# Two graph layers on one core: the exponential of layer 0's source terms moved ahead of their spreading, and a lag of three blocks with eight weight buffers in layer 1

## The chip, the cores and the metric

The kernel runs on one core of a Trainium2 chip. A core has a matrix engine (TensorE, PE in the profile, with its weight loads listed apart as PEld), a vector engine (VectorE, DVE), a scalar engine (ScalarE, ACT), GpSimd (POOL) and SyncE (SP), which only issues transfers here. Each runs its own list of instructions in order, and they wait for each other through semaphores. The metric is the device time of one execution in microseconds (us). Before the change the median of three runs is 3651.67 us (3650.04 to 3655.39).

## The reference, cut to what matters

For 16 graphs of 1024 nodes with 256 features, two layers run one after the other.

```python
# layer 0: 4 heads of 64, one adjacency type in use (adj is 0 or 1)
h      = x @ W                                     # per head
weight = leaky_relu(e_src[i] + e_dst[j], 0.01)     # where adj is 1, else -1e9
dst    = softmax(weight) @ h + bias
out    = head_norm(relu(dst) + h);  x = layer_norm(x + out)
# layer 1: 8 heads of 32, q = k = v = the normalised x
normed = layer_norm(x) * gamma1 + beta1
attn   = softmax(where(adj > 0, normed @ normed.T / sqrt(32), -inf))
y      = x + attn @ normed
y      = y + gelu(layer_norm(y) @ W1 + b1) @ W2 + b2
x      = layer_norm(x + y)
```

In layer 0 the weight before the softmax depends on a source term and a destination term only. exp(leaky_relu(s + d)) is, up to a factor for each destination that is put into the values, the larger of exp(0.99 s) and exp(-0.99 d). So the kernel never takes an exponential of a full 1024 x 1024 matrix in layer 0: it takes those of the terms and forms a maximum. Layer 1 does take an exponential for every pair of nodes and head.

## The kernel before, in words

The 16 graphs ("batches") go through two streams of work. `layer0` (L728) prepares batch b+1 and runs its attention while `layer1` (L745) runs attention and the MLP of batch b. Both are Python generators; every `yield` gives a cost in units of the author's planner. The loop at L789 takes the next piece of layer 0 when its progress is behind what `wanted` (L776) asks for at the present point of layer 1, else the next piece of layer 1. Short side jobs ("chains", such as a normalisation) are begun with a waiting time (`begin`, L270) and resumed by `advance` (L280) once that many units have passed; `complete` (L286) runs what is left of one at once. The order in which the four engines issue is the order in which this program emits; nothing is reordered later. The sums use `ATTN1` (L772), the units of layer 1's attention, so they change if that number does.

**Layer 0.** `prepare` (L312) takes two blocks of 128 nodes at a time: it transposes x (L253), turns the adjacency into a byte mask (L321 on PE, L322 on ACT), forms h and the two terms in one product (L348), and takes from it, on ACT, the source terms (`apart`, L349), the exponentials of the destination terms (L350, L351) and the scaled values (L353). `take_h` (L373, a chain begun 1.5 units after L348) copies h out of the PSUM bank on DVE, and with that the bank is free. `turn_sources` (L365) transposes the source terms and copies them to `esr` (L369).

`attention0` (L376) runs 16 steps for each batch. `spread_factor` (L383) multiplies a row of `esr` with a matrix of ones, so that the source term of every node lies on all 128 partitions (L389), in two PSUM banks of the pool `ps_s`; ACT takes the exponential of them (L391) into `cb`. There are four such pairs for a batch. `weights` makes the masked maximum (L400, DVE), `products` multiplies it with the values (L415, PE). `after0` (L458) is a long chain of normalisations; its last part needs GpSimd for a power (L224), then DVE (L234, L501, L502), then ACT (L240), and ends with transposes (L515, which profile as L253 on PE and L259 on ACT) into nT and with the values v1 (L520) of layer 1. The transposes use banks of the pool `ps_a` (two banks, `acc`), which L321, L348, L253, L368 and L619 share.

**Layer 1.** `attention1` (L528) has 32 steps per batch: two halves of queries, two groups of four heads, eight blocks of 128 keys. Step i is:

- `exponentials(i)`: four products for the logits (L543, below "QK"), one in each of the four banks of `ps_s`, and four exponentials on ACT (L548) into two buffers of the pool `six`;
- `masked(i-1)`: two multiplications with the mask on DVE (L554);
- `products(i-2)` (below "PV"): two heads with the values as the stationary operand (L561), two with the weights as the stationary operand (L568).

The 2 in the last line is `LAG` (L576). The first `LAG` steps cost 1.0 unit each, all others 2.5, and at the end `LAG` more steps have products but no logits. Step 4 is the first to need the second half of the keys. If layer 0's chain for that half has not ended by then, `half` calls `finish_norms` (L722), which completes it on the spot, ahead of QK4.

`heads_out` (L600) divides by the sums, `finish1` (L625) normalises (L630 to L646), `mlp` (L655) runs the two matrix products with a Gelu between (L663, L670, L676), and `last_norm` (L704) normalises once more and writes the result out.

**Buffers.** Pools have a fixed number of buffers for each name: `six` has 6 of the masked weights p, `three` 3 of v1, `four` 4 of z, `two` 2 of relu. A tile that finds no free buffer makes its first writer wait for the last reader of the tile before.

Of the kernel before, what the change touches and what calls it, by code (L numbers as in the profile page):

```python
# [31 lines left out]
F32 = mybir.dt.float32  # L32
# [3 lines left out]
AF = mybir.ActivationFunctionType  # L36
# [3 lines left out]
P = 128  # L40
# [10 lines left out]
def fast_path(  # L51
# [24 lines left out]
    nc = tc.nc  # L76
    B, N, D = x.shape
    H0, _, HO = w0.shape
    T = a_src.shape[2]
    DFF = w1.shape[1]  # L80
    H1 = 8
    HD = D // H1
    NB = N // P
    DC = D // P
    FC = DFF // P
    HALF = 512
    NH = N // HALF
    BPH = HALF // P
    Q = 32
    TILE = 64  # L90
    PAIR = 2
    GB = 2
    QUAD = 4
# [6 lines left out]
    one = ctx.enter_context(tc.tile_pool(name="one", bufs=1))  # L100
    two = ctx.enter_context(tc.tile_pool(name="two", bufs=2))
    three = ctx.enter_context(tc.tile_pool(name="three", bufs=3))
    four = ctx.enter_context(tc.tile_pool(name="four", bufs=4))
    six = ctx.enter_context(tc.tile_pool(name="six", bufs=6))
    small = ctx.enter_context(tc.tile_pool(name="small", bufs=3))
    ps_s = ctx.enter_context(tc.tile_pool(name="ps_s", bufs=4, space=PSUM))
    ps_a = ctx.enter_context(tc.tile_pool(name="ps_a", bufs=2, space=PSUM))
# [62 lines left out]
    bias0_r = rows(nc.scalar, bias0, "bias0_r")  # L170
    for i, (_, _, dst) in enumerate(terms):
        for c in range(DC):
            t = two.tile([P, H0, HO], F32, name="z")
            for pair in range(H0 // PAIR):
                heads = slice(pair * PAIR, (pair + 1) * PAIR)
                nc.vector.tensor_mul(
                    t[:, heads, :],
                    w0e[:, c, pair * P : (pair + 1) * P].rearrange("p (h e) -> p h e", e=HO),
                    vectors[i * PAIR + pair][:, :, :, 0],
                )  # L180
            nc.vector.tensor_reduce(dst[:, c, :], t, axis=mybir.AxisListType.X, op=OP.add)
# [60 lines left out]
    def side_bank(shape):  # L242

        if place[1][1] < ATTN1:
            return ps_a.tile(shape, F32, name="acc")
# [119 lines left out]
    def turn_sources(dst):  # L365
        es = ps_a.tile([P, GB, P], F32, name="acc")
        for g in range(GB):
            nc.tensor.transpose(es[:, g, :], apart[g].rearrange("p h q -> p (h q)"), ident)  # L368
        nc.scalar.copy(dst, es.rearrange("p g q -> p (g q)"))  # L369
        yield from ()  # L370

    def take_h(h, ph):
# [3 lines left out]
    def attention0(b, hb, v0, esr, dinv, factors, mask, rinv):  # L376

        groups = [(n, pair) for n in range(NH) for pair in range(H0 // PAIR)]  # L380
        steps = [(n, hd, j4) for n in range(NH) for hd in range(H0) for j4 in range(0, NB, 4)]

        def spread_factor(n, pair):  # L383

            cb = two.tile([P, PAIR, HALF], F32, name="cb")
            pbs = [ps_s.tile([P, HALF], F32, name="ps") for _ in range(PAIR)]
            for e in range(PAIR):
                q = slice((pair * PAIR + e) * Q, (pair * PAIR + e + 1) * Q)
                nc.tensor.matmul(pbs[e], spread[q, :], esr[q, n * HALF : (n + 1) * HALF], start=True, stop=True)  # L389
            for e in range(PAIR):  # L390
                nc.scalar.activation(cb[:, e, :], pbs[e], AF.Exp, scale=0.99)  # L391
            return cb

        def weights(n, hd, j4):
            ps = []
            cb = cbs[n, hd // PAIR]
            for j2 in (j4, j4 + 2):
                p = four.tile([P, 2, HALF], F32, name="p0")
                for i in range(2):
                    nc.vector.scalar_tensor_tensor(  # L400
                        p[:, i, :],
                        cb[:, hd % PAIR, :],
                        dinv[:, j2 + i, hd : hd + 1],
                        mask[n][:, j2 + i, :],
                        op0=OP.max,
                        op1=OP.mult,
                    )
                ps.append(p)
            return ps

        def products(ps, hd, j4, av):
            for i in range(4):
                for q in range(BPH):
                    for at in range(0, P, TILE):
                        nc.tensor.matmul(  # L415
                            av[at : at + TILE, q, :],
                            ps[i // 2][:, i % 2, q * P + at : q * P + at + TILE],
                            v0[:, j4 + i, hd, :],
                            start=j4 + i == 0 and q == 0,
                            stop=j4 + i == NB - 1 and q == BPH - 1,  # L420
                        )

        cbs = {groups[0]: spread_factor(*groups[0])}
        yield 1.0
        nc.vector.tensor_copy(factors, v0[:, :, :, HO])
        ps = weights(*steps[0])
        yield 1.0
        for i, (n, hd, j4) in enumerate(steps):
            if j4 == 0:
                av = ps_a.tile([P, BPH, HO + 1], F32, name="acc")  # L430
            products(ps, hd, j4, av)
            if i + 1 < len(steps):
                ps = weights(*steps[i + 1])
            if j4 == 0 and i + 3 < len(steps) and hd % PAIR == PAIR - 1:
                g = steps[i + 3][0], steps[i + 3][1] // PAIR
                cbs[g] = spread_factor(*g)
            if j4 == NB - 4:
                norms[b, n, hd] = after0(b, n, hd, av, hb[n], rinv[:, n * BPH : (n + 1) * BPH, :])
                begin(norms[b, n, hd], 2.5)
            yield 2.0  # L440

    def relu_residual(av, hd, hb, rinv):

        nc.vector.reciprocal(rinv[:, :, hd], av[:, :, HO])  # L444
        t = two.tile([P, BPH, HO], F32, name="relu")
        for q in range(BPH):
            nc.vector.scalar_tensor_tensor(
                t[:, q, :],
                av[:, q, 0:HO],
                rinv[:, q, hd : hd + 1],  # L450
                nbias0_r[:, hd * HO : (hd + 1) * HO],
                op0=OP.mult,
                op1=OP.max,
            )
        h = hb[:, :, hd * HO : (hd + 1) * HO]
        nc.vector.tensor_add(h, h, t)

    def after0(b, n, hd, av, o, rinv):  # L458
# [40 lines left out]
        t = minus_mean(mv[:, :, 0], r2[:, 0:BPH], BPH)  # L499
# [14 lines left out]
        for g in range(0, BPH, GB):  # L514
            transpose_rows(nT[:, :, g * P : (g + GB) * P], normed[:, g : g + GB, :], g1_c, be1_c)  # L515
            yield 1.5
        v1 = three.tile([P, BPH, H1, HD + 1], F32, name="v1")
        nc.vector.memset(v1[:, :, :, HD], 1.0)
        for g in range(BPH):
            nc.vector.tensor_mul(  # L520
# [7 lines left out]
    def attention1(half, mask, rinv, done):  # L528
# [8 lines left out]
        def exponentials(n, quad, jb):  # L537
            keys = slice(jb % BPH * P, (jb % BPH + 1) * P)
            of_keys, of_queries = half(jb // BPH)[2], half(n)[2]
            tiles = [ps_s.tile([P, HALF], F32, name="ps") for _ in range(QUAD)]  # L540
            for e in range(QUAD):
                q = slice(e * HD, (e + 1) * HD)
                nc.tensor.matmul(tiles[e], of_keys[q, quad, keys], of_queries[q, quad, :], start=True, stop=True)  # L543
            ps = []
            for e in range(0, QUAD, PAIR):
                p = six.tile([P, PAIR, HALF], F32, name="p")
                for i in range(PAIR):
                    nc.scalar.activation(p[:, i, :], tiles[e + i], AF.Exp, scale=SCALE1)  # L548
                ps.append(p)
            return ps  # L550
# [22 lines left out]
                            stop=jb == NB - 1 and e == PAIR - 1 and q == BPH - 1,  # L573
                        )

        LAG = 2  # L576
        ready = {}
        for i in range(len(steps) + LAG):
            if i < len(steps):
                ready[i] = exponentials(*steps[i])  # L580
            if 0 <= i - 1 < len(steps):
                masked(*steps[i - 1], ready[i - 1])
            if i < LAG:
                yield 1.0
                continue
            n, quad, jb = steps[i - LAG]
            if jb == 0:
                moved = ps_o.tile([P, HALF], F32, name="po")
                held = ps_o.tile([P, BPH, PAIR, HD + 1], F32, name="po")
            products(quad, jb, ready.pop(i - LAG), moved, held)  # L590
            if jb == NB - 1:
# [110 lines left out]
            yield 3.5  # L702

    def last_norm(b, k, po, x1):  # L704
        z = four.tile([P, 1, D], F32, name="z")
        nc.vector.tensor_add(z[:, 0, :], po, x1)
        mv = small.tile([P, 2], F32, name="mv")
        statistics(z[:, 0, :], mv)
        v = small.tile([P, 1], F32, name="v")
        nc.vector.tensor_scalar(v, mv[:, 1:2], EPS, None, op0=OP.add)  # L710
        r = power(v, 1, "r")
        yield 3.5
        t = minus_mean(mv[:, 0:1], r, 1)
        yield 1.5
        scale_shift(z, z, t, r, 1)
        nc.sync.dma_start(out[b, k * P : (k + 1) * P, :], z[:, 0, :])
# [52 lines left out]


    WORK0 = NB // GB * 3.25 + 2.0 + NB * H0 // 2 * 2.0
    ATTN1 = 2.0 + 2.5 * (NH * NB * H1 // QUAD)  # L772
    WORK1 = ATTN1 + NB // GB * (1.75 * FC / 2 + 3.5 * GB)
    COURSE = [(0.0, 1.0), (ATTN1, 1.45), (WORK1 - 14.0, 2.0), (WORK1, 2.0)]

# [469 lines left out]
```

## Time and profile before

One execution was profiled. Its own time and its span, from the first to the last instruction, stand beside the runs:

| | us |
|---|---|
| runs, median (lowest to highest) | 3651.67 (3650.04 to 3655.39) |
| profiled execution, own time | 3651.19 |
| its span | 3649.4 |
| PE busy | 3449.4 |
| DVE busy | 2988.7 |
| ACT busy | 2155.9 |
| POOL busy | 384.4 |
| ACT table loads: before L670, L391, L548, L256 | 46, 30, 15, 1 times 1.283 each |

A line of the costliest groups reads: source line, engine, operation, names of what is written and read, shape, how often; then busy time in us and mean ns of one; then the engine's idle time just before, and what ended it. In the chain of waits, a line names who waited for whom: us in total, times, longest. A line of the timeline gives start, duration, engine, source line, operation, how many were merged, and in brackets the idle time before it with its releaser. A line of the table by stages gives the stretch, its length, then busy us with the number of instructions for PE, PEld, DVE, ACT and POOL, then the clock granted to TensorE, the share of the DMA engines, and GB/s. The ends of matmuls are modelled: a matmul that waits behind another counts as busy, so the busy time of PE holds stalls too.

### The profile page before, as it was taken

How to read it: one execution, taken by the hardware profiler on the slowest of the kernel's cores; microseconds unless marked ns; L12 is line 12 of the kernel's file. 1: busy time of each engine (PE TensorE's matmuls, PEld its weight loads, DVE VectorE, ACT ScalarE, POOL GpSimd, SP SyncE). 2: the span in 40 equal slices, each digit the busy share in tenths (PEclk: the TensorE clock that was granted, in tenths of full speed). 3: DMA queues.
4: the chain of work that ended last, by engine and by line, in shares of the span. 5: the costliest groups of instructions: out<-in, count | busy, mean ns of one | idle time of the engine just before them, and what ended most of it. 6: DMA issues, size and time to landing. Idle time of an engine off the chain costs nothing.

```text
span 3649.4 us, 142033 instructions
## 1 busy us (share of the span) xinstructions
PE 3449.4 (95%) x64417; PEld 2302.3 (63%) x64417; DVE 2988.7 (82%) x5332; ACT 2155.9 (59%) x4732; POOL 384.4 (11%) x360
## 2 busy tenths in 40 slices
PE   6699999999999999999999999999999999999998
PEld 5457576675756757566584765757567575665846
DVE  5788887888878888798887978888788887888884
ACT  3564746647475573755738466474664747557464
POOL 0102011010110101101010010101101011010110
PEclk9899999999999999999999999999999999999999
DMA  4100201011020110201102010020201102010000
GB/s 105 35 16 26 36 12 40 13 30 32 14 43 10 34 27 15 44 9 36 23 16 46 8 42 15 26 36 13 41 11 31 31 14 46 7 38 9 15 7 14
DMA packets 77814, 97.55 MB, mean 27 GB/s; under 512 B 9104, under 2 KB 60048, under 8 KB 77200
## 3 DMA queue, kind: packets, MB, share of 16 engines
q0 software_dynamic: 18432, 33.56, 6.5%
q1 hardware_dynamic: 57184, 53.76, 4.8%
q8 instruction: 506, 8.29, 0.9%
q10 hardware_dynamic: 1584, 1.05, 0.1%
q14 instruction: 108, 0.88, 0.1%
HBM read 105.13 MB, written 16.78 MB: 33 GB/s over the span
## 4 chain that ended last, share of the span: by engine, by line
PE 64%; DVE 25%; issue 4%; ACT 3%; POOL 3%; DMA 1%; SPq 0%; ACTq 0%; POOLq 0%; DVEq 0%
PE ps L543 13%; PE po L561 10%; PE ps L663 9%; PE acc L415 9%; DVE p L554 7%; PE po L676 7%; PE po L568 6%; DVE p L400 6%; PE acc L348 3%; POOL r L224 3%; DVE st L229 2%; PE acc L321 1%; PE acc L253 1%; PE ps L389 1%; DVE mv L230 1%
## 5 line engine op out<-in xcount | busy, mean ns | idle before, releaser
L554 DVE TENSOR_TENSOR p<-p,mask 128x1024 f32<-128x1024 f32 x1024 | 1199.3, 1218 | 161.2 <-ACT p L548 157.3
L548 ACT ACTIVATE p<-ps 128x512 f32<-128x512 f32 x2048 | 1059.6, 614 | 331.7 <-PE ps L543 329.9
L543 PE MATMUL ps<-nT 32*128 32x512 f32 x4096 | 770.1, 655 | 12.6 <-ACT cb L391 10.0
L400 DVE SCALAR_TENSOR_TENSOR p<-cb,dinv,mask 128x512 f32<-128x512 f32 x1024 | 698.5, 744 | 0.9 <-ACT cb L391 0.9
L568 PEld LDWEIGHTS po<-v,p 128*32 128x32 f32 x32768 | 389.4, 109 | 335.0 <-issue 239.3
L415 PE MATMUL acc<-v,p 128*64 128x65 f32 x16384 | 556.1, 226 | 42.1 <-DVE p L400 40.1
L415 PEld LDWEIGHTS acc<-v,p 128*64 128x64 f32 x16384 | 512.0, 139 | 114.3 <-DVE p L400 61.6
L670 ACT ACTIVATE hid<-ps,b_sb 128x256 f32<-128x256 f32 x512 | 235.5, 471 | 556.9 <-PE ps L663 556.5
L561 PE MATMUL po<-p,v 128*32 128x512 f32 x2048 | 548.3, 610 | 10.5 <-DVE p L554 8.8
L561 PE MATMUL po<-p,unit 128*32 128x512 f32 x2048 | 547.9, 610 | 0.0
L663 PE MATMUL ps<-yT,w_sb 128*128 128x256 f32 x2048 | 491.0, 387 | 0.4 <-issue 0.4
L676 PE MATMUL po<-w_sb,hid 128*128 128x256 f32 x2048 | 465.0, 381 | 0.0
L676 PEld LDWEIGHTS po<-w_sb,hid 128*128 128x128 f32 x2048 | 385.4, 190 | 64.0 <-issue 11.4
L663 PEld LDWEIGHTS ps<-yT,w_sb 128*128 128x128 f32 x2048 | 375.6, 190 | 64.9 <-issue 13.1
L568 PE MATMUL po<-v,p 128*32 128x33 f32 x32768 | 387.7, 198 | 9.5 <-issue 4.3
L543 PEld LDWEIGHTS ps<-nT 32*128 32x128 f32 x4096 | 268.2, 186 | 171.1 <-issue 56.9
L561 PEld LDWEIGHTS po<-p,v 128*32 128x32 f32 x2048 | 78.6, 109 | 388.3 <-DVE p L554 206.1
L224 POOL TENSOR_TENSOR r<-v,mhalf 128x1 f32<-128x1 f32 (+1 forms) x160 | 158.1, 988 | 1009.1 <-DVE v L710 721.6
L348 PE MATMUL acc<-w0e,xT 128*128 128x264 f32 x512 | 146.4, 409 | 29.5 <-DVE hb L373 20.9
L322 ACT ACTIVATE mask<-acc,shift_c 128x1024 uint8<-128x1024 bf16 x128 | 144.3, 1127 | 43.6 <-PE acc L321 42.8
L304 POOL DMA_DIRECT2D ak<-in_adj_dram x128 | 69.7, 544 | 862.7 <-PE acc L321 840.3
L224 POOL TENSOR_TENSOR r<-v1s,mhalf 128x4 f32<-128x4 f32 x32 | 34.9, 1090 | 1134.6 <-DVE ranges L444 894.6
(117 smaller groups left out, 2927.9 us busy)
## 6 DMA issues: line engine op xcount, KB each, us to landing
ak<-in_adj_dram POOLq DMA_DIRECT2D x128, 256.0 KB, 3.9
xk<-in_x_dram SPq DMA_DIRECT2D x64, 256.0 KB, 2.8
xl<-in_x_dram SPq DMA_DIRECT2D x32, 512.0 KB, 4.0
out_dram<-z SPq DMA_DIRECT2D x128, 128.0 KB, 1.7
w_sb<-in_L_gnn_W_dram SPq DMA_DIRECT2D x2, 1024.0 KB, 8.0
v<-in_L_gnn_a_src_dram SPq DMA_DIRECT2D x2, 320.0 KB, 4.8
v<-in_L_gnn_a_dst_dram ACTq DMA_DIRECT2D x1, 320.0 KB, 5.0
xl<-in_L_gnn_a_dst_dram ACTq DMA_DIRECT2D x1, 320.0 KB, 5.3
```

Source lines behind the costliest of these rows:

```text
L224: nc.gpsimd.tensor_tensor(r, src, mhalf[:, :n], op=OP.pow)
L348: nc.tensor.matmul(ph, xT[:, c, g * P : (g + 1) * P], w0e[:, c, :], start=c == 0, stop=c == DC - 1)
L400: nc.vector.scalar_tensor_tensor(p[:, i, :], cb[:, hd % PAIR, :], dinv[:, j2 + i, hd : hd + 1], mask[n][:, j2 + i, :], op0=OP.max, op1=OP. ...
L415: nc.tensor.matmul(av[at : at + TILE, q, :], ps[i // 2][:, i % 2, q * P + at : q * P + at + TILE], v0[:, j4 + i, hd, :], start=j4 + i == 0 ...
L543: nc.tensor.matmul(tiles[e], of_keys[q, quad, keys], of_queries[q, quad, :], start=True, stop=True)
L548: nc.scalar.activation(p[:, i, :], tiles[e + i], AF.Exp, scale=SCALE1)
L554: nc.vector.tensor_mul(p, p, mask[n][:, jb, None, :].to_broadcast([P, PAIR, HALF]))
L561: nc.tensor.matmul(moved[at * Q : (at + 1) * Q, :], v, ps[0][:, e, :], start=jb == 0, stop=jb == NB - 1)
L568: nc.tensor.matmul(held[at : at + Q, q, e, :], ps[1][:, e, q * P + at : q * P + at + Q], values[:, hd, :], start=jb == 0 and e == 0 and q ...
L663: nc.tensor.matmul(ph, w1_sb[:, c, f * P : (f + 1) * P], yT[:, c, q * P : (q + GB) * P], start=c == 0, stop=c == DC - 1,)
L670: nc.scalar.activation(hid[f // 4][:, f % 4, :], ph, AF.Gelu, bias=b1_sb[:, f : f + 1], scale=1.0)
L676: nc.tensor.matmul(po, hid[f // 4][:, f % 4, g * P : (g + 1) * P], w2_sb[:, f, :], start=f == 0, stop=f == FC - 1,)
```

## The change

1. In `turn_sources` the copy of the transposed source terms to `esr` becomes an exponential with scale 0.99; in `spread_factor` the exponential becomes a copy. Since the spreading only repeats a row, the result in `cb` stands for the same quantity.
2. In `attention1`, `LAG` becomes 3: step i now multiplies the weights of step i-3. The pool of masked weights gets 8 buffers of 4 KB on each partition rather than 6. `ATTN1` becomes 3.0 + 2.5 x 32 = 83 rather than 82.
3. To make room, v1 gets 2 buffers rather than 3, relu 1 rather than 2, and z 3 rather than 4; the z of the start, which had its own two, shares those of `last_norm`.

```diff
-    six = ctx.enter_context(tc.tile_pool(name="six", bufs=6))
+    eight = ctx.enter_context(tc.tile_pool(name="eight", bufs=8))
...
-            t = two.tile([P, H0, HO], F32, name="z")
+            t = three.tile([P, H0, HO], F32, name="z")
...
-        nc.scalar.copy(dst, es.rearrange("p g q -> p (g q)"))
+        nc.scalar.activation(dst, es.rearrange("p g q -> p (g q)"), AF.Exp, scale=0.99)
...
-                nc.scalar.activation(cb[:, e, :], pbs[e], AF.Exp, scale=0.99)
+                nc.scalar.copy(cb[:, e, :], pbs[e])
...
-        t = two.tile([P, BPH, HO], F32, name="relu")
+        t = one.tile([P, BPH, HO], F32, name="relu")
...
-        v1 = three.tile([P, BPH, H1, HD + 1], F32, name="v1")
+        v1 = two.tile([P, BPH, H1, HD + 1], F32, name="v1")
...
-                p = six.tile([P, PAIR, HALF], F32, name="p")
+                p = eight.tile([P, PAIR, HALF], F32, name="p")
...
-        LAG = 2
+        LAG = 3
...
-        z = four.tile([P, 1, D], F32, name="z")
+        z = three.tile([P, 1, D], F32, name="z")
...
-    ATTN1 = 2.0 + 2.5 * (NH * NB * H1 // QUAD)
+    ATTN1 = 3.0 + 2.5 * (NH * NB * H1 // QUAD)
```

## The prediction

> **What bounds the kernel now.** Page first, then the waits, then one batch in order of time.
>
> ```profile
> PE 3449.4 (95%) x64417; PEld 2302.3 (63%) x64417; DVE 2988.7 (82%) x5332; ACT 2155.9 (59%) x4732; POOL 384.4 (11%) x360
> L554 DVE TENSOR_TENSOR p<-p,mask 128x1024 f32<-128x1024 f32 x1024 | 1199.3, 1218 | 161.2 <-ACT p L548 157.3
> L548 ACT ACTIVATE p<-ps 128x512 f32<-128x512 f32 x2048 | 1059.6, 614 | 331.7 <-PE ps L543 329.9
> L543 PE MATMUL ps<-nT 32*128 32x512 f32 x4096 | 770.1, 655 | 12.6 <-ACT cb L391 10.0
> ```
>
> TensorE looks full, but not all of it is work. 512 steps of L543 (logits, "QK") take 1.50 us each, while an unhindered one takes 1.07.
>
> ```profile
> PE acc L253 <- ACT sq L240: 53.4, 17, 11.0
> PE acc L415 <- DVE p L400: 40.1, 21, 5.0
> PE acc L348 <- DVE hb L373: 20.9, 19, 1.1
> PE po L561 <- DVE p L554: 8.8, 18, 1.7
> ```
>
> The longer lag aims at the last line, PE waiting for masked weights: 8.8 us in all. The others come from layer 0 and from the hand-over between the layers. The TensorE timeline at one hand-over (a batch takes some 222.5 us):
>
> ```profile
> 1249.53 2.59 PE L543 MATMUL ps<-nT 32*128 32x512 f32 x8
> 1252.60 1.97 PE L543 MATMUL ps<-nT 32*128 32x512 f32 x8
> ...
> 1256.05 1.16 PE L348 MATMUL acc<-w0e,xT 128*128 128x264 f32 x4
> 1257.14 1.14 PE L543 MATMUL ps<-nT 32*128 32x512 f32 x8
> ...
> 1259.54 0.77 PE L568 MATMUL po<-v,p 128*32 128x33 f32 x64
> 1262.59 1.92 PE L253 MATMUL acc<-ident,sq 128*128 128x128 f32 x8 [2.28 <-ACT sq L240]
> 1264.52 1.14 PE L543 MATMUL ps<-nT 32*128 32x512 f32 x8
> ```
>
> QK1 and QK2 (2.59, 1.97) hold TensorE because the banks of the previous step are freed only by its four exponentials. Then PE stands 2.28 us for the last piece of layer 0, which step 4 needs. Busy time late in the same attention:
>
> ```profile
> 1319.00:1340.00 21.00, 19.52 (x424) 9.83 (x425) 18.91 (x31) 16.68 (x40) 1.60 (x2) 1.00 0.16 26
> 1340.00:1360.00 20.00, 19.81 (x548) 11.33 (x544) 19.93 (x25) 11.54 (x23) 0.00 (x0) 1.00 0.02 4
> ```
>
> The third column of busy time is VectorE: 19.93 of 20 us. It has no gap from 1321 to 1372, so here two engines run neck and neck.
>
> [...] only L548, L391, L670 and the first L256 are preceded by a load. [...] the rows show 1283, and a load starting 0.01 us after the copy before it, so I use 1.28. [...] in the 15 us from 1030 that hold another hand-over the clock was 0.89.
>
> **Part 1: exponential ahead of spreading.** L391 becomes a copy: 592 ns now, copies of the same size take 594 (L256) and 612 (L603): nothing. L369 becomes an exponential: 371 ns as a copy; a 128x256 Gelu takes 471 (L670), so 0 to 0.1 us x 64, at most 6 us of ACT, beside TensorE; I take 0. Gone are 30 loads before L391 and, Gelu staying loaded, 30 of the 46 before L670: 60 x 1.283 = 77 us of ACT. On the end I value them at 0: ScalarE is idle there. In the MLP the load at 1175.70 is followed by 1.18 us more of waiting for L389, and after the second spread's pair of loads ScalarE waits 4.35 us for L663. No L663 shows a stall there over 0.1 us. The ends: 0 and 77 us.
>
> **Part 2: buffers.** Weights: exp(i) needed products(i-3) done, now i-4; either way TensorE issues those before QK(i): 0. relu has writer and reader on DVE in order: 0. z with three: lives from L706 to its landed write, 1237.46 to about 1244.5; the next L706 are at 1246.01 and 1250.20, so a fourth meets a free one. v1 with two: its last reader ends near 1377, the same half's next write comes with the following batch's layer 0 (as L520 at 1264.5): 0. Were the covers gone, L706 or L518 would hold the masks behind them on DVE, a few us a batch.
>
> **Part 3: the lag, through the planner.** The third start-up step now costs 1.0 rather than 2.5, ATTN1 is 83, so layer 0's pieces fall elsewhere. I followed the planner's sums (they give the timeline's order for before) and then walked PE, ACT and DVE with these durations: QK 1.07, products (PV) 1.56, L321 0.46, L348 1.08, L619 0.59, L415 2.02, four exponentials 2.06, L322 1.1, L349 to L353 1.07, a masked pair 2.36; a QK that waits ends 1.11 after the previous step's exponentials (QK6: 1272.04 to 1273.15).
>
> *Hand-over, before:* QK2, PV0, L348, QK3, PV1, wait, L253 x8, QK4. *After:* QK2, QK3, PV0, L348, wait, L253 x4, L253 x4, QK4. With times from QK0's start (1247.72):
> - QK3 directly follows QK2 at 6.8; exp(2) ends at 9.17 (1256.89), so QK3 ends at 10.3: stall 2.4, was 0.2.
> - PV0 and L348 end at 12.9. The VectorE chain behind L240 sits behind mask(1) and mask(2) as before (to 14.3), so L253 starts at 15.1: wait 2.2, was 2.4 (with 0.3 beside it).
> - L373 of that L348 is now emitted after the transposes; its bank is held, and the second four transposes must take the bank of the first, after L259 (two of about 0.5 us): 17.6. Stall 1.4, was 0. QK4 at 18.2, was 16.8.
>
> Stalls of TensorE in us, from the timeline (before) and the walk (after):
> - Steps 0 to 4: 1.45+0.83+0.19+0.26+2.37 = 5.1; after 1.45+0.83+2.42+2.2+1.4 = 8.3.
> - Steps 5 to 17: 0.81+0.66+0.22+0.66+0.81 = 3.2; after 0.21+0.22+0.30+0.17+0.31+0.76 = 2.0. L321 and L348 now fall in different steps, so fewer steps come bare.
> - Steps 18 to 31: 0.50 + 1.29 (L348 behind L373, itself behind the statistics of L630) + 1.54 + 1.37 (the first spread) + 0.98 + 0.63 + 1.2 (QK31 behind the second spread) = 7.5; after 0.17+0.76+1.3+0.73+0.60 = 3.6. L373 now goes ahead of L630, and the second spread comes after QK31.
>
> Sum 15.8 against 13.9: 1.9 us less per batch. VectorE allows it barely: L609 starts at 78.4 in the walk, with 47.6 us queued to the last mask, so its second half ends at 127.1 and the last PV at 128.0 (before 129.4). Nothing is saved twice: the last PVs carry the product displaced at the start. The MLP's order is unchanged.
>
> 15 batches x 1.9 = 28. The last batch has no layer 0 beside it, so only the lost cover at the start and one product more at the end: +2. Profiled execution 3651.2 (span 3649.4 and 1.8 around it; the median 3651.67 is 0.5 higher): 3651.2 - 26 = 3625.
>
> **Rivals.**
> *A. Slower: the hand-over bank.* The second four transposes get the bank that L373 holds. L373 then stands behind L510, L520 and mask(3) on VectorE and ends at 21.1 rather than 17.5; QK4 waits behind the transposes, and its exponentials with it. For: L348 already waits for L373 (20.9 us, 19 times). Against: at 1324.17 an L321 took the bank freed first, not the oldest. Price 3.5 x 15 = 52: 3678. It decides once the extra wait exceeds the 1.9 gained.
> *B. No change: VectorE paces the tail.* From 1321 it has no gap, so a TensorE freed of stalls waits for masks instead. Against: two masks fewer follow the L630 statistics. 3650.
> *C. The table loads count.* If ScalarE held TensorE in the MLP, 77 us would go: 3574. Against: L670 waits 556.5 us for L663, not the reverse.
> That the lag alone removes mask waits is worth at most the 8.8 us above.
>
> **Chances.** My forecast 0.45, A 0.22, B 0.15, C 0.08, the rest 0.10 (0.06 slower, 0.04 faster). A measurement tells about 0.2% (7 us) from no change: faster 0.45+0.08+0.04 = 0.57, same 0.15, slower 0.22+0.06 = 0.28. The forecast's own range is 3600 to 3642 (a misjudged stall of 1.5 us per batch). To hold 8 in 10 it runs from 3580, short of C, to 3682, past A.
>
> **What would show it.** Right: no load before L391 and 16 before L670; QK3 near 3.5 us long; the eight transposes split by about 1.4 us; PE waiting for L373 far below 20.9; the second spread after the last QK. The sum is wrong if QK4 comes later than 19 after QK0, if L561 waits for L554 more than now, or if the clock sinks at the longer hand-over (each us at half clock costs 0.5).

## The result: 1.0 % slower, and the profile after

The changed kernel takes 3685.93 us (median; 3683.30 to 3694.91) against 3651.07 us for the kernel before: a ratio of 1.0098, 95 % interval [1.0078, 1.0117]. The forecast was 3625, its range ended at 3682. The profiled execution of the changed kernel took 3694.91 us, its span 3693.0; it is the longest of those measured, so sums against it run some 9 us above the median.

The page of the changed kernel, busy times first, then the costliest groups:

```profile
PE 3485.5 (94%) x64417; PEld 2321.3 (63%) x64417; DVE 2990.1 (81%) x5332; ACT 2088.7 (57%) x4672; POOL 398.3 (11%) x360
L554 DVE TENSOR_TENSOR p<-p,mask 128x1024 f32<-128x1024 f32 x1024 | 1201.7, 1219 | 174.6 <-ACT p L548 173.6
L548 ACT ACTIVATE p<-ps 128x512 f32<-128x512 f32 x2048 | 1060.7, 615 | 329.7 <-PE ps L543 327.3
L543 PE MATMUL ps<-nT 32*128 32x512 f32 x4096 | 749.2, 664 | 17.1 <-ACT p L548 15.3
```

TensorE is busy 36 us longer with the same 64417 matmuls, while VectorE's time is what it was and ScalarE has 67 us less. L543 itself fell from 770.1 to 749.2: the logits do wait less. So something else made other matmuls longer: L561, for one, takes 632 ns each where it took 610. The chain of waits, TensorE's own, in us in total, times, longest:

```profile
PE acc L253 <- ACT sq L240: 46.4, 17, 9.8
PE acc L415 <- DVE p L400: 41.0, 22, 5.0
PE acc L253 <- ACT nT L259: 22.5, 16, 1.4
PE po L568 <- DVE o L610: 17.2, 15, 1.2
PE ps L543 <- ACT p L548: 15.3, 17, 1.0
...
PE acc L348 <- DVE hb L373: 4.3, 4, 1.3
```

L561's wait for L554 has gone from 8.8 us to at most 0.1, L348's for L373 from 20.9 to 4.3. Three lines are new or have grown: the second four transposes behind L259 (foreseen, 1.4 us each), QK3 behind the previous exponentials (foreseen, though largely as a stall inside the matmul), and L568 behind L610 (not foreseen). All three together are 55 us, where they were 5 before, while the lines that shrank gave back 42 us (16.6 at L348, 10.0 at L543 behind L391, 8.8 at L561, 7.0 at L253 behind L240). So the waits of TensorE grew by some 8 us, far less than the 36 us by which its busy time grew. What made the same matmuls longer shows in the clock. First a line of the groups by line, on part 1:

```profile
L670 ACT ACT_TABLE_LOAD x16 | 20.5, 1283 | 0.3
```

Part 1 did what it says: 16 loads ahead of L670 instead of 46, and none ahead of L391, which has no row of loads any more. The TensorE timeline of one hand-over (the batch's QK0 is at 1035.00):

```profile
1039.88 1.97 PE L543 MATMUL ps<-nT 32*128 32x512 f32 x8
1042.78 3.53 PE L543 MATMUL ps<-nT 32*128 32x512 f32 x8 [0.93 <-ACT p L548]
...
1047.95 1.11 PE L568 MATMUL po<-v,p 128*32 128x33 f32 x64
1048.99 2.13 PE L348 MATMUL acc<-w0e,xT 128*128 128x264 f32 x4
...
1052.90 0.92 PE L253 MATMUL acc<-ident,sq 128*128 128x128 f32 x4 [1.78 <-ACT sq L240]
1055.27 1.12 PE L253 MATMUL acc<-ident,sq 128*128 128x128 f32 x4 [1.45 <-ACT nT L259]
1056.31 2.09 PE L543 MATMUL ps<-nT 32*128 32x512 f32 x8
```

The order is the one that the prediction walked: QK2, QK3, the products, L348, a wait, four transposes, a wait of 1.45, four more, QK4. But L348 takes 2.13 us where it took 1.16 before, and QK4 2.09 where it took 1.14. The stages of the same hand-over, cut where the clock changes (length; busy us of PE, PEld, DVE, ACT, POOL with their numbers of instructions; clock; DMA share; GB/s):

```profile
1040.75:1044.16 3.41, 2.48 (x11) 1.15 (x8) 3.27 (x10) 3.41 (x8) 0.00 (x0) 1.00 0.37 125
1044.16:1050.98 6.82, 6.82 (x81) 3.04 (x78) 5.22 (x11) 2.73 (x6) 3.10 (x2) 0.50 0.34 57
1050.98:1054.39 3.41, 1.01 (x5) 0.40 (x4) 1.51 (x4) 3.24 (x12) 0.00 (x0) 1.00 0.00 1
1054.39:1061.22 6.83, 5.95 (x86) 2.74 (x87) 6.07 (x11) 3.91 (x8) 0.00 (x0) 0.50 0.01 2
```

TensorE runs at half clock for 6.8 us, at full clock for 3.4 us in which it mostly waits, and again at half clock for 6.8 us. The same table for the kernel before, at the hand-over that begins at 1022.9:

```profile
1036.60:1040.01 3.41, 2.04 (x12) 1.10 (x16) 3.30 (x12) 2.87 (x6) 0.00 (x0) 1.00 0.66 114
1040.00:1043.40 3.40, 3.40 (x30) 0.62 (x30) 3.40 (x7) 2.85 (x7) 0.00 (x0) 0.50 0.00 0
```

It has one stretch of 3.4 us. Over batches 1 to 14 the changed kernel spends 12.9 us at half clock in each hand-over (13.7 in eleven, 10.2 in three), the kernel before 3.2 (3.4 in thirteen, none in one). The mean clock of the whole execution fell from 0.985 to 0.964. QK4 starts 20.9 us after QK0, before 16.9, forecast 18.2; a batch takes 225.0 us, before 222.8, forecast 1.9 less.

### The profile page after: what moved, and what is told of

The parts are those of the page before. It is cut to its first block, busy times and chain, and to the rows that moved or that the text cites. A ratio compares the mean times of both kernels' runs of the same rounds, so it can differ in the third digit from the quotient of the medians.

```text
span 3693.0 us, 141770 instructions
## 1 busy us (share of the span) xinstructions
PE 3485.5 (94%) x64417; PEld 2321.3 (63%) x64417; DVE 2990.1 (81%) x5332; ACT 2088.7 (57%) x4672; POOL 398.3 (11%) x360
## 4 chain that ended last, share of the span: by engine, by line
PE 65%; DVE 23%; ACT 6%; issue 3%; POOL 1%; DMA 1%; SPq 0%; ACTq 0%; POOLq 0%; DVEq 0%
PE ps L543 12%; PE po L561 11%; PE po L676 9%; PE ps L663 9%; PE acc L415 9%; DVE p L400 7%; DVE p L554 7%; PE po L568 6%; PE acc L348 4%; ACT p L548 2%; DVE st L229 2%; PE acc L321 1%; PE acc L253 1%; POOL r L224 1%; PE ps L389 1%
## 5 line engine op out<-in xcount | busy, mean ns | idle before, releaser
L554 DVE TENSOR_TENSOR p<-p,mask 128x1024 f32<-128x1024 f32 x1024 | 1201.7, 1219 | 174.6 <-ACT p L548 173.6
L548 ACT ACTIVATE p<-ps 128x512 f32<-128x512 f32 x2048 | 1060.7, 615 | 329.7 <-PE ps L543 327.3
L543 PE MATMUL ps<-nT 32*128 32x512 f32 x4096 | 749.2, 664 | 17.1 <-ACT p L548 15.3
L400 DVE SCALAR_TENSOR_TENSOR p<-cb,dinv,mask 128x512 f32<-128x512 f32 x1024 | 698.5, 744 | 0.7 <-ACT cb L391 0.5
L568 PEld LDWEIGHTS po<-v,p 128*32 128x32 f32 x32768 | 403.8, 112 | 354.0 <-issue 285.4
L670 ACT ACTIVATE hid<-ps,b_sb 128x256 f32<-128x256 f32 x512 | 237.4, 472 | 594.0 <-PE ps L663 593.9
L561 PE MATMUL po<-p,v 128*32 128x512 f32 x2048 | 569.3, 632 | 0.1
L561 PE MATMUL po<-p,unit 128*32 128x512 f32 x2048 | 568.7, 631 | 0.0
L568 PE MATMUL po<-v,p 128*32 128x33 f32 x32768 | 396.8, 200 | 21.6 <-DVE o L610 17.2
L543 PEld LDWEIGHTS ps<-nT 32*128 32x128 f32 x4096 | 255.7, 188 | 168.1 <-ACT p L548 73.9
L561 PEld LDWEIGHTS po<-p,v 128*32 128x32 f32 x2048 | 79.4, 110 | 385.7 <-issue 206.5
L348 PE MATMUL acc<-w0e,xT 128*128 128x264 f32 x512 | 163.1, 445 | 16.0 <-issue 11.7
L224 POOL TENSOR_TENSOR r<-v1s,mhalf 128x4 f32<-128x4 f32 x32 | 48.4, 1514 | 1111.4 <-DVE ranges L444 807.7
```

Source lines behind the costliest of these rows:

```text
L224: nc.gpsimd.tensor_tensor(r, src, mhalf[:, :n], op=OP.pow)
L348: nc.tensor.matmul(ph, xT[:, c, g * P : (g + 1) * P], w0e[:, c, :], start=c == 0, stop=c == DC - 1)
L400: nc.vector.scalar_tensor_tensor(p[:, i, :], cb[:, hd % PAIR, :], dinv[:, j2 + i, hd : hd + 1], mask[n][:, j2 + i, :], op0=OP.max, op1=OP. ...
L554: nc.vector.tensor_mul(p, p, mask[n][:, jb, None, :].to_broadcast([P, PAIR, HALF]))
L561: nc.tensor.matmul(moved[at * Q : (at + 1) * Q, :], v, ps[0][:, e, :], start=jb == 0, stop=jb == NB - 1)
L568: nc.tensor.matmul(held[at : at + Q, q, e, :], ps[1][:, e, q * P + at : q * P + at + Q], values[:, hd, :], start=jb == 0 and e == 0 and q ...
```

## Experiments: the clock, the bank, the order of the start

Every time is a median, beside runs of the kernel before on the same chip (3647.7 to 3654.1), and the ratio is to those. "Slow windows" are stretches of 3.41 us at half clock, counted over batches 1 to 14 of the one profiled execution, at the hand-over and in the MLP; third_cost has 16 more within the attention. The parts that follow lead through them in the order of the questions.

| kernel | time | ratio, 95 % | mean clock | slow windows, hand-over + MLP |
|---|---|---|---|---|
| before | | 1 | 0.985 | 13 + 5 |
| after | 3685.93 | 1.0098 [1.0078, 1.0117] | 0.964 | 53 + 2 |
| lag2_kept | 3652.61 | 0.9999 [0.9990, 1.0007] | 0.985 | 13 + 3 |
| lag3_alone | 3685.90 | 1.0087 [1.0070, 1.0104] | 0.967 | 49 + 4 |
| bank_free | 3654.66 | 1.0005 [0.9996, 1.0014] | 0.969 | 30 + 13 |
| warm | 3642.03 | 0.9968 [0.9956, 0.9981] | 0.980 | 9 + 13 |
| warm_bank | 3602.78 | 0.9878 [0.9862, 0.9895] | 0.992 | 0 + 0 |
| warm_lag2 | 3643.39 | 0.9986 [0.9977, 0.9995] | 0.987 | 0 + 12 |
| fill_qk3 | 3656.58 | 1.0012 [1.0005, 1.0019] | 0.978 | 20 + 10 |
| fill_late | 3654.36 | 1.0005 [0.9996, 1.0014] | 0.977 | 18 + 11 |
| ramp | 3615.11 | 0.9911 [0.9895, 0.9928] | 0.981 | 14 + 6 |
| ramp_warm | 3596.67 | 0.9848 [0.9832, 0.9864] | 0.988 | 0 + 5 |
| third_cost | 3697.17 | 1.0136 [1.0119, 1.0153] | 0.968 | 18 + 14 |
| warm_mlp | 3629.24 | 0.9935 [0.9918, 0.9951] | 0.987 | 9 + 0 |
| warm_mlp_lag2 | 3633.03 | 0.9945 [0.9928, 0.9961] | 0.992 | 0 + 0 |

### Which part of the change costs?

lag2_kept has the change without the lag; lag3_alone has the lag without the moved exponential.

```diff
 lag2_kept
-        LAG = 3
+        LAG = 2
-    ATTN1 = 3.0 + 2.5 * (NH * NB * H1 // QUAD)
+    ATTN1 = 2.0 + 2.5 * (NH * NB * H1 // QUAD)
 lag3_alone
-        nc.scalar.activation(dst, es.rearrange("p g q -> p (g q)"), AF.Exp, scale=0.99)
+        nc.scalar.copy(dst, es.rearrange("p g q -> p (g q)"))
-                nc.scalar.copy(cb[:, e, :], pbs[e])
+                nc.scalar.activation(cb[:, e, :], pbs[e], AF.Exp, scale=0.99)
```

> The changed kernel with the lag and ATTN1 of before (2 and 82); the moved exponential and the smaller pools stay. If the lag alone makes the loss (at the hand-over), this stands at the time before: 3643 to 3659 us, with 30 table loads fewer before L391. If the moved exponential or the one-buffer relu and two-buffer v1 cost something, it stands between 3665 and 3686. If the table loads counted for TensorE, it stands below 3630.

> The changed kernel with the exponential put back behind the spreading. If the lag makes the loss: 3680 to 3695 us. If the moved exponential makes it: 3640 to 3660. If the table loads hold anything up in this order of work, it is slower than the changed kernel by up to 77 us.

lag2_kept stands at the time of before, lag3_alone at that of after. The whole loss is the lag's. L391 in lag2_kept, from the groups by line:

```profile
L391 ACT COPY cb<-ps 128x512 f32<-128x512 f32 x128 | 68.3, 585 | 154.0 <-PE ps L389 115.3 <-PE ps L543 38.7
```

The 128 copies wait 154.0 us for TensorE: the 60 loads that went (77 us of ScalarE) were taken out of idle time, and gave nothing (0.9999). The smaller pools cost nothing either: the two could have hidden each other here, but after and lag3_alone, which differ in the moved exponential alone, stand together as well. lag3_alone keeps the waits of after: 22.3 us behind L259 and 17.2 behind L610.

### Is it the bank or the clock?

The hand-over contains a wait that leads to another (the bank that `take_h` holds sends the second transposes behind L259) and half-clock stretches. bank_free completes `take_h` ahead of the chain; warm leaves the bank and keeps TensorE occupied with products whose results nobody reads, three of 128x128 ahead of QK3 and seven ahead of the transposes; warm_bank does both.

```diff
 bank_free
-                begin(take_h(hb[-1][:, (k + g) % BPH, :], ph), 1.5)
+                takes[:] = [take_h(hb[-1][:, (k + g) % BPH, :], ph)]
+                begin(takes[0], 1.5)
...
+            if i == BPH and takes:
+                complete(takes[0])
...
+    takes = []
 warm
+        def fill(pool, name, count):
+            t = pool.tile([P, HALF], F32, name=name)
+            for _ in range(count):
+                nc.tensor.matmul(t[:, 0:P], ident, ident, start=True, stop=True)
...
+            if i == LAG:
+                fill(ps_o, "po", 3)
+            if i == BPH:
+                fill(ps_s, "ps", 7)
```

> The changed kernel with one thing more: the copy L373 of the pending block is emitted ahead of step 4, so the second four transposes of the hand-over find their own PSUM bank. The wait of L253 for L259 (22.5 us, 16 times) should go. If that bank is part of the cause: 3645 to 3668 us (1.4 us per batch and part of a half-clock stretch). If the clock has sunk before it anyway and VectorE sets the end of the hand-over: 3680 to 3690.

> The changed kernel with extra products of the identity with itself that nobody reads: three ahead of QK3 and seven ahead of the transposes of the hand-over, where TensorE waits. They add some 2.2 us of TensorE work to each batch, all in idle time. If the sunken clock makes the loss, the half-clock stretches at the hand-over shrink, QK4 starts 19 us or less after QK0 rather than 21.2, and the time falls to 3640 to 3670 us. If the waits alone make it, the time stays at 3680 to 3700.

> The changed kernel with both: the extra products of the identity at the hand-over, read by nobody, and L373 ahead of step 4. If clock and bank are separate terms: QK4 starts near 16.8 us after QK0, and the time is 3615 to 3632 us, faster than before. If one takes the other's place, 3638 to 3652.

Each remedy brings the kernel back to before or a little better; both together bring it to 3602.78. The timeline of warm at one hand-over (QK0 at 1024.48; here L531 is the fill and L548 is QK):

```profile
1036.32 1.16 PE L348 MATMUL acc<-w0e,xT 128*128 128x264 f32 x4
1037.32 1.72 PE L531 MATMUL ps<-ident 128*128 128x128 f32 x14
1039.35 0.93 PE L253 MATMUL acc<-ident,sq 128*128 128x128 f32 x4 [0.31 <-ACT sq L240]
1041.73 1.11 PE L253 MATMUL acc<-ident,sq 128*128 128x128 f32 x4 [1.45 <-ACT nT L259]
1042.78 2.09 PE L548 MATMUL ps<-nT 32*128 32x512 f32 x8
```

L348 is back to 1.16, the first transposes start 14.9 us after QK0, the second 17.3, QK4 18.3 (17.8 to 18.3 over batches 1 to 14; 17.8 in the five without a slow window at the hand-over). The forecast's walk had 15.1, 17.6 and 18.2. The walk of the hand-over is right to about 0.4 us once the clock is what it assumed. In after the first transposes came at 17.9: there L348 takes 2.13 us, ScalarE's L349 to L353 start behind it at 1051.15, and L240, for which the transposes wait, is issued after those and starts at 1052.23, 17.2 after QK0 (in before 14.2). The fills take a PSUM bank each, too, but warm waits as long for its banks as after does (22.7 us behind L259, 17.4 behind the line that is L610 in after), so that is not where it gains.

In warm_bank the eight transposes follow one another again (here L549 is QK):

```profile
1027.29 1.92 PE L253 MATMUL acc<-ident,sq 128*128 128x128 f32 x8 [0.32 <-ACT sq L240]
1029.22 1.14 PE L549 MATMUL ps<-nT 32*128 32x512 f32 x8
```

QK4 comes 16.8 after QK0 (1012.42), as in before, with no slow window in any of the batches 1 to 14.

At 3602.78 us warm_bank is faster than either range that was expected for it. By their ratios, each to the runs beside it, the two remedies add up: against after the bank alone brings 0.93 %, the fills 1.30 %, both together 2.20 %. (The plain times differ by 31, 44 and 83 us, but warm_bank ran on a chip on which the kernel before, too, took 5 us less.) What stays open is which of the two fills does it, and why warm is 17 us above the 3625 that the walk gives.

### Which of the two fills?

fill_qk3 has only the first (ahead of QK3), fill_late only the second.

```diff
 against warm: fill_qk3
-            if i == BPH:
-                fill(ps_s, "ps", 7)
 against warm: fill_late
-            if i == LAG:
-                fill(ps_o, "po", 3)
```

> The changed kernel with only the first of the two fills: three products of the identity with itself ahead of QK3, read by nobody. If the clock falls because TensorE runs four bare logit steps without products, this alone lifts the first half-clock stretch (6.8 us) and brings 20 to 35 of the 44 us: 3651 to 3666. If the idle time ahead of the transposes is what brings it down: 3678 to 3690.

> The changed kernel with only the second fill: seven products of the identity with itself ahead of the transposes, read by nobody. If the bare logit steps bring the clock down, the first stretch stays and TensorE is late by then, so the fill stands in its way: 3670 to 3690. If the wait ahead of the transposes does: 3645 to 3660.

Each alone takes out about two thirds of what both do (0.86 and 0.93 of 1.30 %). That is no sum of two places: with either fill some 33 to 35 of the 53 slow windows at the hand-over go, but 8 or 9 come up in the MLP.

### The lag of two with the same fills

```diff
 against warm: warm_lag2
-        LAG = 3
+        LAG = 2
-    ATTN1 = 3.0 + 2.5 * (NH * NB * H1 // QUAD)
+    ATTN1 = 2.0 + 2.5 * (NH * NB * H1 // QUAD)
```

> The changed kernel with the lag of before (2) and the same extra products at the hand-over, read by nobody. The kernel before has one half-clock stretch of 3.4 us per hand-over. If the clock after the wait costs half of the TensorE work in it, 1.0 to 1.7 us per batch: 3625 to 3640 us. If the shorter stretch cost nothing: 3648 to 3660.

5 us better than before by its ratio, and just above the range of 3625 to 3640 that was expected. Read at once against warm_bank, this says that a lag of three is worth 40 us when no clock is lost. The next two runs show that this reading was wrong.

### Where the missing part is: slow windows that moved into the MLP

In warm, 13 of 14 batches have a slow window in the MLP; in after only two have one. The wait that precedes it is in both, TensorE waiting 1.9 us for the weights of L400. First warm, the window with the wait (1.93 us from 990.89 on) and the next; the columns are those of the stages above:

```profile
990.29:993.70 3.41, 1.48 (x25) 0.96 (x25) 3.11 (x10) 2.79 (x6) 1.05 (x2) 1.00 0.11 39
993.70:997.11 3.41, 3.41 (x53) 3.29 (x50) 3.41 (x7) 0.00 (x0) 0.00 (x0) 0.50 0.00 0
```

Then after, the same wait (1.91 us from 1228.18 on), which the boundary at 1228.48 divides (0.30 us before it, 1.61 after):

```profile
1228.48:1231.89 3.41, 1.80 (x48) 1.57 (x48) 3.31 (x8) 2.31 (x6) 0.92 (x1) 1.00 0.02 5
```

The boundaries are no choice of the reader's. In each of the fifteen traces the changes of the clock lie whole multiples of 3.413 us apart, to within 0.01 us (75 changes in after, 47 in before, 805 in all). This divides each trace into windows, and whether half clock followed the wait went with its place among them. The thirteen kernels without the third fill have 182 such waits of 1.9 to 2.3 us in batches 1 to 14. Of the 88 that lie wholly within one window, 83 were followed by half clock; of the 94 that a boundary cuts, 15 were (in before 3 of 3 and 1 of 10, in after 2 of 14, with none in the first group). Two more kernels take the wait away: warm_mlp adds a third fill ahead of step 13 of layer 0's attention, where that wait is; warm_mlp_lag2 is the same with a lag of two.

```diff
 against warm: warm_mlp
+            if i == 13:
+                fill(ps_s, "ps", 7)
             products(ps, hd, j4, av)
 against warm_mlp: warm_mlp_lag2
-        LAG = 3
+        LAG = 2
-    ATTN1 = 3.0 + 2.5 * (NH * NB * H1 // QUAD)
+    ATTN1 = 2.0 + 2.5 * (NH * NB * H1 // QUAD)
```

> The two fills at the hand-over as before, and a third one (seven 128x128 products whose results nobody reads) ahead of step 13 of layer 0's attention, where TensorE waits 1.93 us for the weights of L400 in the MLP. Theory [...]: with the hand-over warmed, the batch has slipped so that this wait falls inside one window and is followed by one window at half clock in 14 of 15 batches, 3.4 us each, 1.7 us lost; filled, the stretch goes and with it 14 x 1.7 = 24 us: 3618 us, clock 0.99[...]. The forecast's walk at full clock (3625) would then be nearly right. Rival (what was missing to 3625 is the wait for the held output bank and the last batch, and the wait in the MLP costs nothing at either clock): 3642, as without the third fill.

> The same three fills with a lag of two (the change's exponential and buffers kept). Theory: its two-fill twin at 3643 had one half-clock window in the MLP of 12 of 15 batches; without them 12 x 1.7 = 20 us less: 3623 us, clock 0.99. The lag of three then gains nothing by itself against it (3618 to 3625 with its bank wait), and about 20 us once the bank is free (3603). Rival (the lag itself is worth 40 us at full clock): stays at 3643.

The windows in the MLP are gone in both, and both became faster: warm_mlp by 0.33 % (12 us) over warm, warm_mlp_lag2 by 0.41 % (15 us) over warm_lag2. The gains were smaller than expected (24 and 20 us). In part that is because warm's profiled execution, from which I had counted (3647.83 us, clock 0.980), had more half clock than its median run (3642.03, 0.982). The price of a slow window was also a little lower than the 1.7 us that I used: in warm_mlp five batches have none and take 219.6 us on average, nine have one at the hand-over and take 221.3, so there one costs 1.6, and the comparisons of whole kernels below give 1.1 to 1.3. The timeline of warm_mlp at the filled place (L379 is the fill, L420 the products of layer 0):

```profile
990.17 1.73 PE L379 MATMUL ps<-ident 128*128 128x128 f32 x14
992.24 2.67 PE L420 MATMUL acc<-v,p 128*64 128x65 f32 x64 [0.35 <-DVE p L405]
```

The fill lies wholly inside the wait, of which 0.35 us are left, and is not itself in the way.

With that the numbers of the fills add up too. Among the kernels with the lag of three and the held bank, after (55 slow windows) and warm_mlp (9) are 1.63 % or 60 us apart: 1.3 us for a window. This puts lag3_alone (53) at 1.0091, fill_qk3 (30) at 1.0009, fill_late (29) at 1.0006 and warm (22) at 0.9981; measured 1.0087, 1.0012, 1.0005, 0.9968. bank_free (43) and warm_bank (0) are 46 us apart, 1.1 us for a window. What looked like an interplay of the two fills is the number of windows that each kernel loses, hand-over and MLP together.

And the lag itself: with all three fills, lag two has no slow window and a batch takes 221.0 us; lag three takes 219.6 in the batches without one. The lag gains 1.4 us a batch at full clock. Against warm_mlp_lag2 (0.9945) warm_bank (0.9878) gains 0.67 %, 24 us: that much is the lag of three with the bank free, not 40.

### Other ways to start

The cheap steps at the start are 0 to 2 rather than 0 and 1, so that QK3 directly follows QK2 and TensorE has little beside logits there. ramp keeps two, begins the products at step 2, and goes over to a lag of three by leaving out the products at step 6. third_cost leaves the order and only gives the third step its old price in the planner's units.

```diff
 ramp
-        LAG = 3
+        LAG, SKIP = 3, 6
-            if i < LAG:
+            if i < LAG - 1 or i == SKIP:
                 yield 1.0
                 continue
-            n, quad, jb = steps[i - LAG]
+            at = i - LAG + (i < SKIP)
+            n, quad, jb = steps[at]
...
-            products(quad, jb, ready.pop(i - LAG), moved, held)
+            products(quad, jb, ready.pop(at), moved, held)
 third_cost
-                yield 1.0
+                yield 2.5 if i == LAG - 1 else 1.0
-    ATTN1 = 3.0 + 2.5 * (NH * NB * H1 // QUAD)
+    ATTN1 = 4.5 + 2.5 * (NH * NB * H1 // QUAD)
 ramp_warm: ramp, and ahead of the exponentials
+            if i == LAG - 1:
+                fill(ps_o, "po", 3)
+            if i == BPH:
+                fill(ps_s, "ps", 7)
```

> The changed kernel with the lag growing from 2 to 3 after the hand-over: products start at step 2 as before, and step 6 issues none (1.0 unit). The hand-over then runs in the order of before. If the loss lies in the hand-over alone: 3615 to 3640 us. If it lies in the longer lag as such (VectorE, the last steps): 3665 to 3690.

> The changed kernel with the third start-up step at 2.5 units rather than 1.0 (ATTN1 84.5): layer 0's L348 falls ahead of QK3 again and L373 ahead of the transposes, but PV0 and PV1 still come later than before. If the order of layer 0's pieces makes the loss: 3640 to 3660 us. If the missing products do (TensorE without work, clock down): 3670 to 3700.

> The version whose lag grows from 2 to 3 after the hand-over, with the two fills (products of the identity with itself, read by nobody). It ran at 3615 with one half-clock stretch of 3.4 us per hand-over. If each stretch costs what it did with lag 2 (9 us in all without it): 3600 to 3612. If the fills are in the way: 3615 to 3625.

ramp, without any work added, is 0.89 % faster than before: one slow window at each hand-over as before, the wait behind L259 gone, and the logits' stalls of the later steps saved. L561 waits for L554 in all 1.7 us. ramp_warm, at 3596.67 us, is the fastest of all, 1.5 % under before, and below the 3600 to 3612 that was expected.

third_cost restores the hand-over (QK4 at 16.8) and is nevertheless the slowest. Its chain of waits shows why:

```profile
PE po L568 <- DVE o L610: 41.3, 15, 2.8
PE acc L368 <- DVE o L610: 25.1, 15, 1.7
```

Layer 0's pieces fall elsewhere for the 1.5 units, and 66 us of waits for VectorE's L610 come up: 1.7 us at L368, some 49 us after QK0, and 2.8 us at L568, some 109 us after it. The second leaves TensorE with little to do in one window (from 1140.28 on: 0.65 us of PE busy in 3.41), and the next, from 1143.69 on, is at half clock. This happens in each of batches 1 to 14, so that third_cost has 48 slow windows in all, 30 more than before. Its 3697 lies in the range expected for it, but the work that was missing is not that of the hand-over.

## Why the prediction was wrong

**The step that failed** is the walk of the hand-over, "QK4 at 18.2, was 16.8": it was made with durations at full clock. Its order, its waits and, with the clock held (warm), its times are right; with the clock as it was, QK4 came at 20.9. The text named the case among what would make it wrong ("if the clock sinks at the longer hand-over") and gave it no term in the sum. At 1.3 us a window, 55 slow windows rather than 18 are 48 us, while warm_mlp against warm_mlp_lag2, with warm_mlp's nine windows (15 us at 1.6) taken off, says that the rest of the change is worth 3614 - 3633 = -19 us. Together +29; measured +35. The 1.3 comes from two of these kernels, so this is a check of the sum and no second proof. The price that the text gave, 0.5 for each us at half clock, was nearly right: 1.1 to 1.6 us for a window of 3.41 is 0.3 to 0.5. What it had wrong is that it counted no such window. The signs in the trace were there: the 0.89 over another hand-over was quoted and left as a remark, though a stage with the clock at 0.50 for 3.4 us lay at the hand-over in 13 of the batches 1 to 14 of before, and the new order lengthened just the stall that precedes it. The hand-over that was walked, from 1247.72 on, happens to be the only one of batches 1 to 14 without such a stage:

```profile
1247.72:1266.00 18.28, 15.55 (x213) 7.23 (x216) 17.78 (x42) 15.72 (x37) 4.12 (x4) 1.00 0.27 73
```

TensorE was not without work in the windows ahead of half clock. Of those printed above, the four that half clock followed have PE idle for 0.93 and 2.40 us of 3.41 (after), 1.37 (before) and 1.93 (warm); the one in after with 1.61, from 1228.48 on, kept the full clock.

**Its other terms.**
- *Stalls of steps 5 to 31*, forecast 10.7 to 5.6: the shape is right. QK4 to the start of QK31 took 106.3 us, now 102.1.
- *The wait behind L259*, 1.4 us, 16 times: right to 0.05 us.
- *"VectorE allows it barely"*: mis-sized. L568 of the products of step 24 waits for L610 in each batch, 17.2 us in all, before 2.9: VectorE reaches `heads_out` too late for TensorE's next bank. This is 1.0 us a batch, and at full clock the batch gains 1.4 rather than 1.9. It is rival B at one place, not for the whole tail.
- *The last batch*, +2: it was +5.7 (178.0 to 183.8 us from QK0 to the end). The exponentials of step 24 stand behind L240 on ScalarE, which waits for VectorE's L234, as ScalarE's timeline shows:

```profile
3590.05 2.08 ACT L240 ACTIVATE o<-o,t,r 128x256 f32<-128x256 f32 x4 [2.42 <-DVE t L234]
```

  The clock sinks there too: 0.75 on average from 3588 to 3600, and the L543 step that follows took 3.52 us. It comes with the lag: lag2_kept has 178.2, warm_bank 183.7, ramp 182.9. In part it is the clock: warm_mlp, also with a lag of three but at full clock there, has 180.2.
- *Opening*: the first QK0 at 124.6 rather than 119.4 makes 5 us of the profiled execution; it varies between 120.7 and 124.5 in the other kernels, with lag two as well, and is not the change's.
- *Parts 1 and 2*, nothing: right (0.9999).

**The rivals.** A came nearest in time (3678), and its mechanism did not happen: the second transposes took the bank freed first, L373 came at 1058.36, after both, and only the 1.4 us were paid. B holds at L568 alone. C is excluded by lag2_kept. The chance of a slower kernel was set at 0.28, for the bank and unnamed cases; the clock had no case of its own.

In the sum over the profiled executions: 3694.9 is 70 above the forecast. Opening 5; fifteen batches at 2.2 longer instead of 1.9 shorter, 15 x 4.1 = 61; last batch 4. Of the 4.1, 0.5 is what the lag gains less at full clock, and the other 3.6 is the clock: 37 more windows over 14 batches at 1.3 each are 3.4.

## What to carry to other kernels

When a change puts the bare and waiting steps of TensorE next to one another, walk the stage a second time at half clock: here L348 took 2.13 us rather than 1.16 and QK4 2.09 rather than 1.14, and the waits of TensorE grew by 8 us, its busy time by 36. Look through the trace for the stages at 0.50 before predicting, count them, and treat each as a term. Two edits that seem to interact should be compared by their ratios to the runs beside them, and by their number of slow windows, first; and where a pipeline is made deeper, deepen it after a hand-over (here: leave out a product at step 6, 0.9911) rather than at its start (1.0098).

## What the hardware showed that I had not expected

- **The same wait did not always cost a slow window.** The half-clock stretches counted here are 3.41 us long or a multiple of it: in batches 1 to 14 of before 18 of one window each, in after 30 with 55 windows. Of the waits of 1.9 to 2.3 us, half clock followed 83 of 88 that lay within one window and 15 of 94 across a boundary.
- **Neither busy time shown here settles which windows half clock followed.** Over batches 1 to 14, of the windows at full clock with PE busy for 2.0 to 2.6 us (where a stalled matmul counts as busy) 4 of 31 in before and 12 of 35 in after were followed by half clock; of those with under 0.9 us of weight loads (PEld) 9 of 16 and 14 of 27. What decides it was not shown.
- **One place can lose its clock batch after batch**: the MLP in 12 or 13 of 14 batches of bank_free, warm and warm_lag2. In warm_bank a boundary cuts the wait in the MLP in all 14 batches, and no slow window is there; that this is in part a matter of where the wait fell is an estimate from the 83 of 88 and 15 of 94. Why a wait keeps its place from batch to batch was not shown.
- **A few products that nobody reads pay for themselves**: at the hand-over ten of them, 2.7 us of TensorE at a place where it would wait, took out 44 of the 53 windows there (warm against after) and, although 11 came up in the MLP, 44 us (47 by the ratios).
